# Attention scores in 64x64 TensorE tiles instead of 32x128 ones, and some key products of 480 columns for two of 240

## The chip, the cores and the metric

The kernel runs on one core of a Trainium2 chip. The metric is the device time of one execution in microseconds. Everything is float32, and every matrix product of the program appears in the profile as two TensorE records (two MATMUL and two LDWEIGHTS), so that counts in the profile are twice those in the code. The profile calls the matrix product PE, the loading of its stationary operand ("weights") PEld, VectorE DVE, ScalarE ACT, GpSimd POOL and SyncE SP.

## The reference

There are 16 batches of 100 queries with 640 features, and 8 heads of 80 channels. Each batch attends to 718 keys of 384 features (the first 718 of 722 context rows); the last four rows are extra tokens that get an attention of their own. Cut to what matters here:

```python
query = hidden_states @ Wq                # 16 x 100 x 640
keyt  = enc @ Wk                          # 16 x 718 x 640
valt  = enc @ Wv
scores = einsum('bhqd,bhkd->bhqk', qh, kh) * 80 ** -0.5   # 8 heads of 80 channels
hs = softmax(scores) @ vh
# a second, small attention over the 4 tokens gives ca_hs2
out = (hs + ca_hs2) @ Wout + b_out + hidden_states
```

## The kernel before

**Setup.** `load_heads` (L301) and the DMA behind it (L308, chunk 4) bring the transposed key weights into the room of `kT`, the heads in 32-row pieces, on the DMA queues of ACT and SP. `turn_back` transposes five chunks of 128 channels on TensorE, and `first_keys` makes the keys of batch 0: for each chunk and each 128 features of the context it multiplies three thirds of the keys, 240 columns each (L620). ACT rearranges the query weights from `wq_in` into `wq_sb` with three copies for each of five row chunks (L1279, L1287).

**Channels.** Of each head's 80 channels the first 64 lie in chunks 0 to 3 of `kT` and of the queries `qp`, and the other 16 in chunk 4 (`qz` on the side of the queries). In the kernel before the 64 channels are cut into two pieces of 32 rows: head h has rows 32(h//2) onward of chunks 2(h%2) and 2(h%2)+1. In chunk 4 each head has 16 rows; `qz` holds each query twice with one or the other 16 rows of a 32-row block zeroed, so that one product with 200 columns serves two heads.

**Scores.** For each batch the function `scores` runs three times (groups g = 0, 1, 2), each for two tiles of 120 keys. Inside it, for each key tile and each of the five chunks, four products follow each other, one for each 32-row block r, and each goes to a PSUM bank of its own (L660): stationary are 32 rows x 120 keys of `kT`, moving are 32 rows x 100 queries (chunks 0 to 3) or x 200 columns of `qz` (chunk 4). The four use four separate row tiles of the array (32 rows x 128 columns), and the text below calls four such records with different tiles a quad. Groups 0 and 2 write to two double banks (pool `ps2`), which ACT copies to the tile `st` with one instruction each (L688); group 1 writes to four single banks, copied with four (L682). VectorE takes the running maximum over `st` (`most`: L1416, then `larger`, L1407).

**The rest of a batch.** The order on each engine is the order of the code (the schedule is manual). Behind the scores PE does the small second attention (`z_ps`, `y_ps`), then the values of this batch and the keys of the next in turns (L439, L470: block products that need fewer multiplications, with sums that POOL, DVE and ACT make), while DVE and ACT compute the softmax (`Maximum`, `subtract` L1395, `exponential` L1403). `last_keys` (through `chunk_keys`, L568) makes chunk 4 of the next batch's keys: three thirds of 240 columns times three times 128 features. Every second batch the queries of two batches follow (L544). Then come the products with the probabilities: `r_ps` (L1546, four column tiles of 32) for the last channels of each head and the sum of the probabilities, and `a_ps` (L1564, two column tiles of 64). Behind `a_ps` the next batch's scores follow at once. In batches 1, 3, 5, 11, 13 and 15 an exponential of the second attention (L854) stands on ACT between the copies of group 0 and those of group 1; in batch 0 it stands behind those of group 1.

The lines that the change touches in the product itself:

```python
for a in range(2):
    for c in range(HC):                      # five chunks
        for r in range(RG):                  # four row blocks of 32
            rows = slice(32 * r, 32 * r + 32)
            if c < HC - 1:
                rhs = qp[rows, c // 2, c % 2, (b % 2) * S : (b % 2 + 1) * S]
                product(a, c, rows, r, c // 2 * S, rhs, False)
            else:
                product(a, c, rows, r, 0, qz[rows, 0, b % 2], True)
```

Of the kernel before, what the change touches and what calls it, by code (L numbers as in the profile page):

```python
# [15 lines left out]
NH, D = 8, 80  # L16
# [131 lines left out]
def kernel(  # L148
# [121 lines left out]

    def a_form(enc, f):
        return enc[0][:, A_AT[f]]
# [26 lines left out]
    def load_heads(u):  # L299
        for h in range(u, NH, 2):  # L300
            (nc.scalar, nc.sync)[h // 2 % 2].dma_start(**packed(wkt_sb, wkt, h))  # L301
# [6 lines left out]
    nc.sync.dma_start(  # L308
        out=wkt_sb[:, 4], in_=wkt.rearrange("(h k) n -> h k n", h=NH)[:, 64:]
    )  # L310
# [252 lines left out]
    def chunk_keys(n, banks, weights, enc):  # L563
        copies = []
        for bank, thirds in zip(banks, ((0, 1), (2,))):
            for i, u in enumerate(thirds):
                for c in range(CC):
                    nc.tensor.matmul(  # L568
                        bank[:, i * KT : (i + 1) * KT],
                        weights[c],  # L570
                        a_raw(enc, u, c),
                        start=(i == 0 and c == 0),
                        stop=(c == CC - 1),
                        skip_group_check=True,
                    )
# [21 lines left out]
    def first_keys(enc):  # L597
# [14 lines left out]
        for c, chunks in ((0, (0, 1)), (0, (2, 3)), (1, range(4)), (2, range(4))):  # L612
            if len(banks) < 4 and 2 in chunks:
                for n in (2, 3, 4):
                    turn_back(n, copies[n % 2])
                begin(2, psum1)
                begin(3, psumk)
            for n in chunks:
                for u in range(3):
                    nc.tensor.matmul(  # L620
                        banks[n][u // 2][:, u % 2 * KT : (u % 2 + 1) * KT],
                        wk_sb[:, 2 * c + n % 2, n // 2],
                        a_raw(enc, u, c),
                        start=(u != 1 and c == 0),
                        stop=(c == CC - 1),
                        skip_group_check=True,
                    )
# [8 lines left out]
    def last_keys(b, enc):  # L636
        banks = pair(f"kT_ps_{b}")
        return chunk_keys(
            HC - 1,
            [banks[:, k] for k in range(2)],  # L640
            [wk4[:, c] for c in range(CC)],
            enc,
        )


    def scores(b, g, tiles):
# [11 lines left out]
        def product(a, c, rows, bank, lo, rhs, last):  # L658
            u, j = KC[2 * g + a]
            nc.tensor.matmul(  # L660
                s_ps[bank][:n, 256 * a + lo : 256 * a + lo + rhs.shape[-1]],
                kT[rows, c, u, j * KN : (j + 1) * KN],
                rhs,
                start=bank not in opened,
                stop=last,
                skip_group_check=True,
            )
            opened.add(bank)
# [608 lines left out]
    for c in range(HC):  # L1277
        for u in range(2):
            nc.scalar.copy(  # L1279
                wq_sb[:, c, 2 * u * P : 2 * (u + 1) * P].rearrange(  # L1280
                    "p (v r k) -> p r v k", v=2, r=RG
                ),
                wq_in[c].rearrange("p (r u k) -> p r u k", r=RG, u=2)[
                    :, :, u, :64
                ].rearrange("p r (v k) -> p r v k", v=2),
            )
        nc.scalar.copy(  # L1287
            wq_sb[:, c, 4 * P :].rearrange("p (h k) -> p h k", h=NH),
            wq_in[c].rearrange("p (h k) -> p h k", h=NH)[:, :, 64:],
        )  # L1290
# [56 lines left out]
    last_keys(0, enc)  # L1347
# [29 lines left out]
    for b in range(B):  # L1377
# [55 lines left out]
        if b + 1 < B:  # L1433
# [62 lines left out]
            last_keys(b + 1, enc)  # L1496
# [45 lines left out]
        for i in order:  # L1542
            for e in range(2):
                for h in range(e, NH, 2):
# [4 lines left out]
                        st[i // 2][: KEYS[i], i % 2, h * S : (h + 1) * S],  # L1549
# [11 lines left out]
        for i in range(len(KC)):  # L1561
            for h in range(NH):
# [4 lines left out]
                    st[i // 2][: KEYS[i], i % 2, h * S : (h + 1) * S],  # L1567
# [66 lines left out]
```

## Time and profile before

| | |
|---|---|
| median of 3 runs | 921.77 us (920.55 to 922.27) |
| the profiled execution | 921.04 us, its span 919.3 us |
| PE busy, PEld busy | 912.0 us (99%), 776.6 us (84%) |
| DVE, ACT, POOL busy | 665.5 us (72%), 376.6 us (41%), 620.6 us (68%) |
| granted clock | 1.00 throughout |
| share of the scores (L660) in the chain that ended last | 12% |

The profile gives one execution. The chain that ended last is followed back from the last instruction; the groups by line give busy time and the mean duration of one record; the timeline merges records of one kind that follow each other and gives the start of the first, the time until the end of the last and their count. A record's duration contains the time in the pipeline, so that rates are read here from the distance of starts and not from durations: the scores of batch 1 start at 95.32 us, and the next stage at 102.60 us.

### The profile page before, as it was taken

How to read it: one execution, taken by the hardware profiler on the slowest of the kernel's cores; microseconds unless marked ns; L12 is line 12 of the kernel's file. 1: busy time of each engine (PE TensorE's matmuls, PEld its weight loads, DVE VectorE, ACT ScalarE, POOL GpSimd, SP SyncE). 2: the span in 40 equal slices, each digit the busy share in tenths (PEclk: the TensorE clock that was granted, in tenths of full speed). 3: DMA queues.
4: the chain of work that ended last, by engine and by line, in shares of the span. 5: the costliest groups of instructions: out<-in, count | busy, mean ns of one | idle time of the engine just before them, and what ended most of it. 6: DMA issues, size and time to landing. Idle time of an engine off the chain costs nothing.

```text
span 919.3 us, 26076 instructions
## 1 busy us (share of the span) xinstructions
PE 912.0 (99%) x11155; PEld 776.6 (84%) x11155; DVE 665.5 (72%) x1121; ACT 376.6 (41%) x654; POOL 620.6 (68%) x653
## 2 busy tenths in 40 slices
PE   8999999999999999999999999999999999999998
PEld 8988889797887979888798788988888888888865
DVE  3898795979639696675957759579782887828773
ACT  2354533544324443433434334344541445425351
POOL 9665786677847788476774756755796566955735
PEclk9999999999999999999999999999999999999999
DMA  9604351141402313140221403205140151401312
GB/s 288 218 11 133 66 123 34 29 120 39 103 12 70 106 25 90 43 132 12 72 72 43 132 12 81 71 6 134 43 110 11 34 140 36 111 11 45 86 53 64
DMA packets 68060, 69.50 MB, mean 76 GB/s; under 512 B 25192, under 2 KB 61352, under 8 KB 67944
## 3 DMA queue, kind: packets, MB, share of 16 engines
q1 hardware_dynamic: 67016, 66.97, 27.2%
q8 instruction: 88, 1.44, 0.7%
q10 hardware_dynamic: 464, 0.52, 0.2%
q0 software_dynamic: 464, 0.34, 0.2%
q14 instruction: 28, 0.23, 0.1%
HBM read 62.14 MB, written 8.94 MB: 77 GB/s over the span
## 4 chain that ended last, share of the span: by engine, by line
PE 97%; DMA 1%; POOL 1%; ACT 0%; DVE 0%; issue 0%; ACTq 0%; SPq 0%; DVEq 0%; POOLq 0%
PE s_ps L660 12%; PE v_psA L439 11%; PE v_psB L439 9%; PE k_psA L470 8%; PE a_ps L1564 7%; PE q_ps L544 7%; PE k_psB L470 7%; PE kT_ps L568 6%; PE r_ps L1546 4%; PE v_psC L439 4%; PE k_psC L470 3%; PE y_ps L799 2%; PE v_psD L439 2%; PE o_psy L1128 2%; PE v_psE L439 2%; PE k_psE L470 1%
## 5 line engine op out<-in xcount | busy, mean ns | idle before, releaser
L834 POOL TENSOR_TENSOR e<-ca,g 100x800 f32<-100x800 f32 x60 | 91.8, 1540 | 101.0 <-DVE most L1407 74.3
L439 PE MATMUL v_psA<-wv_sb,enc 128*120 128x320 f32 x384 | 119.6, 434 | 0.0
L507 POOL TENSOR_TENSOR enc<-enc 128x240 f32<-128x240 f32 x144 | 108.7, 765 | 8.0
L439 PE MATMUL v_psB<-wv_sb,enc 128*120 128x320 f32 x320 | 99.2, 432 | 0.0
L660 PE MATMUL s_ps<-qp,kT 32*120 32x100 f32 x3072 | 97.4, 263 | 0.0
L660 PEld LDWEIGHTS s_ps<-qp,kT 32*120 32x120 f32 x3072 | 94.7, 179 | 1.9
L841 POOL TENSOR_TENSOR e<-e,e 100x800 f32<-100x800 f32 x45 | 92.2, 2048 | 3.5
L439 PEld LDWEIGHTS v_psA<-wv_sb,enc 128*120 128x120 f32 x384 | 69.0, 183 | 24.7 <-DVE vs L410 0.9
L1395 DVE TENSOR_TENSOR st<-st,over 120x1600 f32<-120x1600 f32 x46 | 88.8, 1930 | 0.0
L470 PE MATMUL k_psA<-enc,wk_sb 128*128 128x240 f32 x360 | 87.6, 366 | 0.0
L470 PEld LDWEIGHTS k_psA<-enc,wk_sb 128*128 128x128 f32 x360 | 68.4, 190 | 17.1
L1407 DVE TENSOR_TENSOR most<-most,st 120x800 f32<-120x800 f32 x64 | 63.3, 990 | 21.7 <-ACT st L682 20.4
L439 PEld LDWEIGHTS v_psB<-wv_sb,enc 128*120 128x120 f32 x320 | 58.6, 183 | 23.4
L1403 ACT ACTIVATE st<-st 120x1600 f32<-120x1600 f32 x48 | 73.9, 1540 | 8.2 <-DVE st L1395 5.7
L470 PE MATMUL k_psB<-enc,wk_sb 128*128 128x240 f32 x300 | 73.0, 366 | 0.0
L1416 DVE TENSOR_TENSOR most<-st 120x800 f32<-120x800 f32 x16 | 17.3, 1082 | 76.6 <-ACT st L688 76.6
L1564 PE MATMUL a_ps<-st,vs 120*64 120x100 f32 (+1 forms) x1536 | 69.5, 250 | 0.0
L544 PE MATMUL q_ps<-xT,wq_sb 128*128 128x200 f32 x400 | 69.1, 332 | 0.0
L1564 PEld LDWEIGHTS a_ps<-st,vs 120*64 120x64 f32 (+1 forms) x1536 | 66.4, 137 | 2.7 <-issue 2.7
L544 PEld LDWEIGHTS q_ps<-xT,wq_sb 128*128 128x128 f32 x400 | 68.0, 190 | 0.2
L412 ACT COPY vs<-v_psA 120x640 f32<-120x640 f32 x48 | 33.3, 693 | 83.8 <-PE v_psA L439 83.7
L688 ACT COPY st<-s_ps 120x800 f32<-120x800 f32 x64 | 49.7, 829 | 43.4 <-PE s_ps L660 43.4
(183 smaller groups left out, 1886.2 us busy)
## 6 DMA issues: line engine op xcount, KB each, us to landing
pb<-p_d SPq DMA_DIRECT2D x32, 400.0 KB
enc<-in_enct SPq DMA_DIRECT2D x30, 240.0 KB
enc<-in_enct SPq DMA_DIRECT2D x15, 360.0 KB
xT<-in_xt SPq DMA_DIRECT2D x8, 500.0 KB
rest<-in_enct SPq DMA_DIRECT2D x31, 120.0 KB
xn<-in_x SPq DMA_DIRECT2D x11, 320.0 KB
wide_d<-p_d SPq DMA_DIRECT2D x16, 200.0 KB
pb<-wide_d SPq DMA_DIRECT2D x16, 200.0 KB
```

The costliest lines, as they stand in the source:

```text
L439: nc.tensor.matmul(at[0][j][:KN, : H // 2], a_form(self.enc, f)[:, j * KN : (j + 1) * KN], wv_sb[:, W_AT[f]], start=first, stop=last, skip ...
L470: nc.tensor.matmul(at[:, i * KT : (i + 1) * KT], wk_sb[:, W_AT[f], i], a_form(self.enc, f), start=(first and i == 0), stop=last, skip_grou ...
L507: first = nc.gpsimd.tensor_tensor(out, left, right, op)
L544: nc.tensor.matmul(q_ps[:, : 2 * S].rearrange("p (j s) -> p j s", j=2), wq_sb[:, c, n * P : (n + 1) * P], xT[:, :, c, :], start=(c == 0), ...
L568: nc.tensor.matmul(bank[:, i * KT : (i + 1) * KT], weights[c], a_raw(enc, u, c), start=(i == 0 and c == 0), stop=(c == CC - 1), skip_group ...
L660: nc.tensor.matmul(s_ps[bank][:n, 256 * a + lo : 256 * a + lo + rhs.shape[-1]], kT[rows, c, u, j * KN : (j + 1) * KN], rhs, start=bank not ...
L834: first = engine.tensor_tensor(to, self.ca[:, t, :].unsqueeze(1).to_broadcast([S, NH, S]), g[:, :, t].unsqueeze(2).to_broadcast([S, NH, S] ...
L841: engine.tensor_tensor(e, e, to, ALU.add)
L1395: return engine.tensor_tensor(st[i], st[i], top.over[:KN].unsqueeze(1).to_broadcast([KN, 2, ROWS]), ALU.subtract,)
L1403: nc.scalar.activation(st[i], st[i], AF.Exp, scale=SCALE)
L1407: most_now = nc.vector.tensor_tensor(most[:KN], most[:KN], st[i][:, u], ALU.max)
L1564: nc.tensor.matmul(wides[64 * e : 64 * e + 64, h // 2], slot(i, h, FIRST[e], 64), st[i // 2][: KEYS[i], i % 2, h * S : (h + 1) * S], start ...
```

## The change

The first 64 channels of a head now lie together: chunk c holds head 2c in rows 0 to 63 and head 2c+1 in rows 64 to 127. The heads stand in `st` in another order (`PLACE`: first the even heads, then the odd), and the readers of `st` follow it. In `scores` each product with 32 rows x 120 keys becomes one with 64 rows and half of the keys: the stationary operand is 64 rows x 64 keys, or x 56 for the second half, and the four products of a quad use the four 64x64 tiles of the array (two row halves times two column halves). Their number stays: 32 products of 100 columns in a group. The products of chunk 4 keep their form (32 rows x 120 keys, 200 columns, eight in a group), but they no longer stand between those of the key tiles: all products of the heads are together (`heads`), and all of chunk 4 are together (`others`). Groups 0 and 2 do the heads first, group 1 does chunk 4 first, so that the order in a batch is heads, chunk 4 (of groups 0 and 1), heads (of groups 1 and 2), chunk 4.

In `first_keys`, in `last_keys(0)` and in the loop's `last_keys` of batches 6 and 7, the products of the first two thirds of the keys are joined to one with 480 moving columns for the second and third 128 features; the first 128 features stay apart, since one third lies in another tile there. That makes 14 products of 480 columns out of 28 of 240. In the calls of `last_keys` that join, the loop over the features is now the outer one.

In the setup the loads of the key weights go in pieces of 64 rows, the four heads of chunks 0 and 1 first; that of chunk 4 becomes two DMAs on SP's queue instead of one. The query weights take two copies on ACT for each row chunk instead of three.

```diff
+PLACE = [4 * (h % 2) + h // 2 for h in range(NH)]
 def packed(to, w, h):
     rows = w.rearrange("(h k) n -> h k n", h=NH)
-    at, c = 32 * (h // 2), 2 * (h % 2)
-    return {
-        "out": to[at : at + 32, c : c + 2],
-        "in_": rows[h, :64].rearrange("(v k) n -> k v n", v=2),
-    }
+    return {"out": to[64 * (h % 2) : 64 * (h % 2) + 64, h // 2], "in_": rows[h, :64]}
...
     def load_heads(u):
-        for h in range(u, NH, 2):
-            (nc.scalar, nc.sync)[h // 2 % 2].dma_start(**packed(wkt_sb, wkt, h))
+        for h in range(4 * u, 4 * u + 4):
+            (nc.scalar, nc.sync)[h % 2].dma_start(**packed(wkt_sb, wkt, h))
...
-    nc.sync.dma_start(
-        out=wkt_sb[:, 4], in_=wkt.rearrange("(h k) n -> h k n", h=NH)[:, 64:]
-    )
+    for e in range(2):
+        nc.sync.dma_start(
+            out=wkt_sb[64 * e : 64 * e + 64, 4],
+            in_=wkt.rearrange("(c e k) n -> e c k n", e=2, k=D)[e, :, 64:],
+        )
...
+    def a_two(enc, c):
+        at = A_RAW[0, c]
+        return enc[0][:, at : A_RAW[1, c] + 1 : A_RAW[1, c] - at]
...
+    def raw_keys(banks, c, weights, enc, joined=True):
...
+        if joined and (1, c) not in A_REST:
+            product(banks[0], 0, a_two(enc, c), False)
+        else:
+            for u in range(2):
+                product(banks[0], u * KT, a_raw(enc, u, c), u == 0 and c == 0)
+        product(banks[1], 0, a_raw(enc, 2, c), c == 0)
...
-        for a in range(2):
-            for c in range(HC):
+        def heads(last):
+            for a in range(2):
+                for c in range(HC - 1):
+                    for e in range(2):
+                        at = 4 * e + c
+                        rows = slice(64 * e, 64 * e + 64)
+                        rhs = qp[rows, c // 2, c % 2, (b % 2) * S : (b % 2 + 1) * S]
+                        for keys in (slice(0, 64), slice(64, n)):
+                            product(a, c, rows, keys, at // 2, at % 2 * S, rhs, last)
+
+        def others(last):
+            for a in range(2):
                 for r in range(RG):
                     rows = slice(32 * r, 32 * r + 32)
-                    if c < HC - 1:
-                        rhs = qp[rows, c // 2, c % 2, (b % 2) * S : (b % 2 + 1) * S]
-                        product(a, c, rows, r, c // 2 * S, rhs, False)
-                    else:
-                        product(a, c, rows, r, 0, qz[rows, 0, b % 2], True)
+                    product(a, HC - 1, rows, slice(0, n), r, 0, qz[rows, 0, b % 2], last)
+
+        for k, part in enumerate((others, heads) if g == 1 else (heads, others)):
+            part(k == 1)
...
     for c in range(HC):
-        for u in range(2):
-            nc.scalar.copy(
-                wq_sb[:, c, 2 * u * P : 2 * (u + 1) * P].rearrange(
...
+        nc.scalar.copy(
+            wq_sb[:, c, : 4 * P].rearrange("p (h k) -> p h k", h=NH),
+            wq_in[c].rearrange("p (h k) -> p h k", h=NH)[:, :, :64],
+        )
...
-    last_keys(0, enc)
+    last_keys(0, enc, True)
...
-            last_keys(b + 1, enc)
+            last_keys(b + 1, enc, b in (6, 7))
...
-                        st[i // 2][: KEYS[i], i % 2, h * S : (h + 1) * S],
+                        st[i // 2][: KEYS[i], i % 2, PLACE[h] * S : (PLACE[h] + 1) * S],
```

More of the change, by code (lines that the diff above doesn't have):

```diff
@@ L560, in queries, with product, chunk_keys @@
                 )
-    def chunk_keys(n, banks, weights, enc):
-        copies = []
[L565 to L575, printed above, removed]
+    def raw_keys(banks, c, weights, enc, joined=True):
+        def product(bank, lo, rhs, first):
+            cols = rhs.shape[-1] * (rhs.shape[1] if len(rhs.shape) > 2 else 1)
+            to = bank[:, lo : lo + cols]
+            if len(rhs.shape) > 2:
+                to = to.rearrange("p (u k) -> p u k", k=KT)
+            nc.tensor.matmul(
+                to,
+                weights,
+                rhs,
+                start=first,
+                stop=(c == CC - 1),
+                skip_group_check=True,
+            )
[5 more added lines that the diff above has]
+        product(banks[1], 0, a_raw(enc, 2, c), c == 0)
+    def chunk_keys(n, banks, weights, enc, joined):
+        copies = []
+        if joined:
+            for c in range(CC):
+                raw_keys(banks, c, weights[c], enc)
+        else:
+            for bank, thirds in zip(banks, ((0, 1), (2,))):
+                for i, u in enumerate(thirds):
+                    for c in range(CC):
+                        nc.tensor.matmul(
+                            bank[:, i * KT : (i + 1) * KT],
+                            weights[c],
+                            a_raw(enc, u, c),
+                            start=(i == 0 and c == 0),
+                            stop=(c == CC - 1),
+                            skip_group_check=True,
+                        )
         for bank, thirds in zip(banks, ((0, 1), (2,))):
@@ L618, in first_keys @@
             for n in chunks:
[L619 to L627, printed above, removed]
+                raw_keys(banks[n], c, wk_sb[:, 2 * c + n % 2, n // 2], enc)
         for n in banks:
@@ L634, in first_keys, with last_keys @@
                 )
-    def last_keys(b, enc):
+    def last_keys(b, enc, joined=False):
         banks = pair(f"kT_ps_{b}")
@@ L656, in scores, with product @@
         opened = set()
-        def product(a, c, rows, bank, lo, rhs, last):
+        def product(a, c, rows, keys, bank, lo, rhs, last):
             u, j = KC[2 * g + a]
+            first = [k for k in (0, 64) if keys.start <= k < keys.stop and (bank, k) not in opened]
             nc.tensor.matmul(
-                s_ps[bank][:n, 256 * a + lo : 256 * a + lo + rhs.shape[-1]],
-                kT[rows, c, u, j * KN : (j + 1) * KN],
+                s_ps[bank][keys, 256 * a + lo : 256 * a + lo + rhs.shape[-1]],
+                kT[rows, c, u, j * KN + keys.start : j * KN + keys.stop],
                 rhs,
-                start=bank not in opened,
+                start=bool(first),
                 stop=last,
```

16 lines of the change are left out of this document (6 added, 10 removed).

## The prediction

> **What bounds the kernel now.** I read the page first: busy shares and the chain that ended last.
>
> ```profile
> span 919.3 us, 26076 instructions
> ...
> PE 912.0 (99%) x11155; PEld 776.6 (84%) x11155; DVE 665.5 (72%) x1121; ACT 376.6 (41%) x654; POOL 620.6 (68%) x653
> ...
> PE 97%; DMA 1%; POOL 1%; ACT 0%; DVE 0%; issue 0%; ACTq 0%; SPq 0%; DVEq 0%; POOLq 0%
> ```
>
> The chain is PE for 97% of the span: PE's own stream sets the end, and a stage is worth what its records take from start to start. So next the timeline of PE around the scores of batch 1 (start, time to the end of the last, record, count), and the groups by line for the weight loads.
>
> ```profile
> 88.54 0.37 PE L568 MATMUL kT_ps<-rest,wk 128*128 128x240 f32 x1
> 88.83 2.28 PE L1546 MATMUL r_ps<-st,vs 120*32 120x100 f32 x96
> 91.05 4.35 PE L1564 MATMUL a_ps<-st,vs 120*64 120x100 f32 x96
> 95.32 1.10 PE L660 MATMUL s_ps<-qp,kT 32*120 32x100 f32 x32
> 96.24 0.54 PE L660 MATMUL s_ps<-qz,kT 32*120 32x200 f32 x8
> 96.60 1.00 PE L660 MATMUL s_ps<-qp,kT 32*120 32x100 f32 x32
> 97.42 0.54 PE L660 MATMUL s_ps<-qz,kT 32*120 32x200 f32 x8
> ...
> 102.13 0.54 PE L660 MATMUL s_ps<-qz,kT 32*120 32x200 f32 x8
> 102.60 0.75 PE L861 MATMUL z_ps<-y,e 100*32 100x33 f32 x64
> ```
>
> ```profile
> L660 PEld LDWEIGHTS s_ps<-qp,kT 32*120 32x120 f32 x3072 | 94.7, 179 | 1.9
> ...
> L1564 PEld LDWEIGHTS a_ps<-st,vs 120*64 120x64 f32 x1024 | 45.3, 137 | 2.7 <-issue 2.7
> ...
> L1546 PEld LDWEIGHTS r_ps<-st,vs 120*32 120x32 f32 x1024 | 22.6, 110 | 5.7 <-issue 5.0 <-ACT st L1403 0.8
> ...
> L568 PEld LDWEIGHTS kT_ps<-enc,wk 128*128 128x128 f32 x224 | 42.5, 190 | 2.8
> ```
>
> And from the chain in order of time (start, us, records), rows for full-width products and for the last batch:
>
> ```profile
> 32.41 1.69 PE q_ps L544 x10
> ...
> 38.73 6.77 PE q_ps L544 x40
> ...
> 66.39 1.08 PE v_psE L439 x4
> ...
> 85.26 3.65 PE kT_ps L568 x18
> ...
> 104.48 1.10 PE v_psA L439 x4
> ...
> 132.80 3.65 PE kT_ps L568 x18
> ...
> 890.02 1.74 DVE st L1395
> 891.89 7.15 POOL st L1395 x2
> 899.07 1.55 ACT st L1403
> ```
>
> The scores take 102.60 - 95.32 = 7.28 us a batch. A stretch of 32 qp records (8 quads) takes 97.42 - 96.60 = 0.82, so 0.102 a quad: seven spacings of 0.105 and one of 0.085, the latter right behind chunk 4, whose longer stream gave the loads time. What moves in a quad is only 100 columns, and elsewhere such a quad or pair is faster. r_ps is 24 quads from 88.83 to 91.05, 2.22 us; a_ps is 48 pairs from 91.05 to 95.32, 4.27 us. Less the switches below, that is 0.087 and 0.086. Full-width records give the same pace: 200 columns 6.77 / 40 = 0.169, 240 columns 3.65 / 18 = 0.203, 320 columns 1.08 / 4 = 0.270, that is 0.85 ns a column and nearly no offset, so 100 columns are 0.085. The scores thus wait about 0.02 a quad for something else. The loads say for what: their mean goes 110, 137, 179 ns for 32, 64, 120 stationary columns, 0.8 ns a column, so 120 columns occupy a row tile for about 0.100, longer than the 0.085 that the products need; 64 columns take about 0.053.
>
> **The change part by part.**
>
> *Heads, 64x64.* 48 quads a batch as before (3 groups x 32 products x 2 records / 4), each moving 100 columns, but loading at most 64 columns. No 64x64 tile runs in this trace. The bounds are 0.085 (the moving columns) and 0.105 (as now). I take 0.086, a_ps's value: a_ps loads 64 columns into two column tiles beside each other and isn't held up by it, and s_ps shows that row tiles load beside each other too; the change combines the two. 48 x 0.086 = 4.13. That a load runs beside the product before it in the same rows is what a_ps's 0.086 rests on: each of its records uses all rows and brings a load of its own, 0.053 by the columns. [...]
>
> *Chunk 4.* 12 quads of 200 columns, unchanged in form. Two quads now take 96.60 - 96.24 = 0.36, the first of them 0.19; in a row of four or eight I take q_ps's 0.17: 12 x 0.17 = 2.04. At 0.18 it would be 2.15.
>
> *Switching the tile form.* This is what the change adds: heads, chunk 4, heads, chunk 4 have four changes of form behind them in a batch, where the scores had one. Going out costs 0.09 to 0.11: the last kT record starts at 88.54 and r_ps at 88.83, 0.29 where 0.203 is usual; the last chunk-4 stretch takes 102.60 - 102.13 = 0.47 where 0.36 is usual. Coming in costs the first load, which nothing covers: the first qp stretch takes 96.24 - 95.32 = 0.92 against 0.82, so 0.10 for 120 columns; by the columns, 0.05 for 64. Inside a batch: out 4 x 0.11 = 0.44; in, 2 x 0.05 + 2 x 0.10 = 0.30. The way in from a_ps has its going-out share in a_ps's 4.27 before and after, and isn't counted.
>
> *Sum of the scores.* 4.13 + 2.04 + 0.44 + 0.30 = 6.91 against 7.28: 0.37 us less a batch. The faster quads alone save 48 x (0.102 - 0.086) = 0.79, and the three more changes of form give more than half back.
>
> *What the shorter scores run into.* Groups 0 and 2 share their banks, so group 2 waits for two copies; ACT, and DVE's maximum, follow in order:
>
> ```profile
> 98.04 1.55 ACT L688 COPY st<-s_ps 120x800 f32<-120x800 f32 x2 [2.11 <-PE s_ps L660]
> 99.48 0.88 ACT L854 ACTIVATE e<-e 100x800 f32<-100x800 f32 x1
> 100.38 1.68 ACT L682 COPY st<-s_ps 120x400 f32<-120x400 f32 x4
> 102.76 1.55 ACT L688 COPY st<-s_ps 120x800 f32<-120x800 f32 x2 [0.69 <-PE s_ps L660]
> ```
>
> ```profile
> 102.10 2.02 DVE L1407 TENSOR_TENSOR most<-most,st 120x800 f32<-120x800 f32 x2 [1.24 <-ACT st L682]
> ...
> 104.77 2.01 DVE L1407 TENSOR_TENSOR most<-most,st 120x800 f32<-120x800 f32 x2
> ```
>
> The copies of group 0 end at 99.59, and group 2 starts two groups after the first, at 95.32 + 0.92 + 0.36 + 3 x 1.18 = 100.13: 0.54 spare. After the change group 0 ends 2.32 into the stage (heads 0.05 + 16 x 0.086 + 0.11, chunk 4 0.10 + 4 x 0.17), its copies, as long after it as now, at 4.12; group 2 can start at 4.53 (0.68 more of chunk 4, 0.11 out, 0.05 in, 16 x 0.086): 0.41 spare, no wait. In the six batches with L854 there, ACT is full from 98.04 to 102.06, and its copies of group 1, and DVE's next maximum with them, come earlier only by what group 0 gains, 2.46 - 2.32 = 0.14, while PE comes 0.37 earlier. PE has 28 us of values and keys to do (104.48 to 132.80 in this batch) before r_ps needs this softmax, so that costs nothing unless a block product waits for DVE's sums; if that cover is gone, at most the 0.23 in six batches, 1.4 us. In batch 15 the chain does leave PE, for DVE, POOL and ACT (10.4 us in the rows above), and these start from that maximum: there I count 0.1 instead of 0.37. In batch 0 the exponential that z_ps waits for stands behind group 1's copies, which come about 0.6 earlier: 0.2 more than 0.37.
>
> *480 columns for two of 240.* 28 records less. With 0.85 ns a column and an offset of about 2 ns (0.270 for 320 against 0.203 for 240), they save some 2 ns each: 0.06. The upper bound is their loads, 28 x 0.19 = 5.3, if these lay open, but at 0.203 for 240 columns they don't. A moving operand in two pieces costs nothing at q_ps (two pieces of 100, 0.169). The reordered `last_keys` waits for the same double bank.
>
> *Setup.* PE's list of waits, and rows of the timeline:
>
> ```profile
> PE w_ps L589 <- DMA kT<-in_wkt: 0.8, 2, 0.5
> PE m_ps L1321 <- DVE wq L1308: 0.5, 1, 0.5
> ...
> PE z_ps L861 <- ACT e L854: 0.2, 1, 0.2
> ```
>
> ```profile
> 0.82 0.87 SPq L301 DMA_DIRECT2D kT<-in_wkt  x2
> ...
> 4.97 0.78 SPq L308 DMA_DIRECT2D kT<-in_wkt  x1
> ...
> 10.13 0.52 PE L589 MATMUL w_ps<-e,kT 128*128 128x128 f32 x3 [0.50 <-DMA kT<-in_wkt]
> ```
>
> ```profile
> 29.72 0.29 ACT L1287 COPY wq_sb<-wq 128x128 f32<-128x128 f32 x1
> ```
>
> PE stands twice for the key weights, 0.8 in all. Chunk 4 in two DMAs is 2 x 0.435 = 0.87 of issue instead of 0.78, and the second half starts later; whatever SP issues behind it goes 0.1 later. Chunk 0 on the other hand needs two heads instead of four. I take 0, with -0.3 (the wait for the first chunks gone) to +0.5 (the second half lands one issue later). ACT's copies, five fewer, now end at 30.0 and are needed when q_ps starts, at 32.4: nothing.
>
> *Total.* 14 x 0.37 + (0.37 + 0.2) + 0.1 + 0.06 = 5.9. From the profiled execution, 921.04 (the span 919.3 and 1.7 around it), that is 915.1. This execution lies 0.7 below the median of the runs, inside their range, so I predict 915.4.
>
> **The rivals.**
>
> *Column tiles don't load beside each other under row tiles: slower.* If the two column tiles of a row half take turns, 64 + 56 columns are 120 again, and the quad stays at 0.105: heads 48 x 0.105 = 5.04 and the first load 0.10, so the batch is 5.04 + 2.04 + 0.44 + 0.40 = 7.92, 0.64 more, in 15 batches 9.6: 930.6. Where it turns: 0.37 / 48 more than 0.086, that is 0.094 a quad. For it speaks only that this combination is not in the trace; against it a_ps (128 stationary columns in 0.086) and r_ps (four times 32 in 0.087), where turns would need 0.107. 0.10.
>
> [...]
>
> *The gain is eaten by waits and dearer switches.* If each of the four changes of form costs the full 0.11 and 0.10, they take 0.84 instead of 0.74, and 0.27 a batch remains, 16 x 0.27 = 4.3; the waits of the six batches take 1.4 back: 921.04 - 4.3 + 1.4 = 918.1. For it speaks ACT, full in those batches; against it that PE's list of waits has none for DVE or ACT over 0.5 us. 0.10.
>
> *The switches are cheaper between the row-tiled forms.* If nothing drained between tiles of 64 and of 32 rows, the three changes inside a batch would save 0.33 again: 16 x 0.33 = 5.3, 915.4 - 5.3 = 910.1. Both goings-out quoted show the 0.1, so 0.08.
>
> **How the numbers follow.** The forecast has 0.70, with its own range of 913 to 918 (quads at 0.085 or 0.088, chunk 4 at 0.18, setup -0.3 to +0.5). Runs of this kernel spread by 0.2%, about what a measurement can tell from no change. The range reaches over the eaten gain on one side and toward the cheaper switches on the other: 911.5 to 919.5. Faster by more than 0.2% is below 919.9: 0.70 + 0.08 + most of 0.10, so 0.85; slower 0.12; 0.03 remain.
>
> **What would show it.** In the profile after: the scores of a batch take 6.9 us from the first record to z_ps; 64x64 quads start every 0.086; weight loads of 64 columns have a mean near 137 ns; four changes of form with 0.15 to 0.2 each stand between the stretches; kT_ps of batches 6 and 7 keeps 3.6 us with 14 records; q_ps of batch 0 starts at 32.4 as before. It would be wrong if the quads come at 0.1 or more, if z_ps or v_psA wait for ACT's copies, or if the first transposes start much later.

## The result, and the profile after

The changed kernel takes 915.07 us in the median of 6 runs (914.59 to 916.98), the kernel before 921.2 in 6 runs beside it: 0.9938 of its time, with an interval of 0.9928 to 0.9948. It is faster by 0.6%, as forecast, and 0.3 us below the predicted time. The profiled execution took 914.95, its span 913.2 us.

From the page of the profile after: span, busy time, the shares of the chain that ended last, and the weight loads of the scores.

```profile
span 913.2 us, 26025 instructions
...
PE 905.1 (99%) x11127; PEld 756.6 (83%) x11127; DVE 667.6 (73%) x1121; ACT 375.4 (41%) x649; POOL 619.9 (68%) x653
...
PE 94%; DMA 2%; DVE 1%; POOL 1%; ACT 1%; issue 0%; SPq 0%; POOLq 0%; ACTq 0%; DVEq 0%
...
L687 PEld LDWEIGHTS s_ps<-qp,kT 64*56 64x56 f32 (+1 forms) x3072 | 66.9, 130 | 5.9 <-issue 3.9
```

PE's stream still sets the end. The weight loads of the heads' channels have a mean of 130 ns, where those of 120 columns had 179 (the tiles now have 64 or 56). The timeline of PE around the scores of batch 1, in the changed kernel:

```profile
96.25 1.60 PE L687 MATMUL s_ps<-qp,kT 64*64 64x100 f32 x64
97.78 1.63 PE L687 MATMUL s_ps<-qz,kT 32*120 32x200 f32 x32
99.34 2.97 PE L687 MATMUL s_ps<-qp,kT 64*64 64x100 f32 x128
102.24 0.95 PE L687 MATMUL s_ps<-qz,kT 32*120 32x200 f32 x16
103.12 0.83 PE L897 MATMUL z_ps<-y,e 100*32 100x33 f32 x64
```

The scores take 103.12 - 96.25 = 6.87 us instead of 7.28. The four stretches last 1.53, 1.56, 2.90 and 0.88 us from start to start. PE's list of waits after (us in total, how often, the longest):

```profile
PE w_ps L622 <- DMA kT<-in_wkt: 2.3, 2, 1.8
PE idle_ps L1293 <- DVE vaT L1290: 1.1, 1, 1.1
PE m_ps L1352 <- DVE wq L1339: 0.5, 1, 0.5
PE r_ps L1577 <- ACT st L1434: 0.3, 1, 0.3
PE k_ps L1327 <- ACT kT L656: 0.2, 1, 0.2
```

The list of before ended with one more row than the prediction shows:

```profile
PE z_ps L861 <- issue: 0.2, 1, 0.2
```

That is a stall without a cause that the profile names ("issue"). No wait for DVE or ACT is new, and this stall is gone; but the wait for the key weights has grown from 0.8 to 2.3 us. Its place, in the timelines of SP and of PE:

```profile
0.82 1.47 SPq L305 DMA_DIRECT2D kT<-in_wkt  x2
...
5.67 1.26 SPq L313 DMA_DIRECT2D kT<-in_wkt  x2
```

```profile
8.87 0.82 PE L622 MATMUL w_ps<-e,kT 128*128 128x128 f32 x6
11.45 0.52 PE L622 MATMUL w_ps<-e,kT 128*128 128x128 f32 x3 [1.76 <-DMA kT<-in_wkt]
...
48.76 1.43 PE L687 MATMUL s_ps<-qp,kT 64*64 64x100 f32 x56
```

The transposes of chunk 4 start at 11.45 instead of 10.13, `q_ps` of batch 0 at 33.52 instead of 32.24, and the scores of batch 0 at 48.76 instead of 47.49.

Stage by stage, from start to start in the two profiled executions:

| PE's stage | after less before, us |
|---|---|
| setup, up to the scores of batch 0 | +1.27 |
| scores, 16 batches (batch 0 -0.57, each of the others -0.40) | -6.63 |
| `z_ps`, `y_ps` | -0.60, -0.25 |
| values and keys (+0.25 in batch 0), `kT_ps` in the loop | +0.25, -0.02 |
| `r_ps`, `a_ps`, what follows PE's last product | -0.18, +0.13, -0.07 |
| sum | -6.1 |

The scores account for the gain and half a microsecond more. Against them stands the loss in the setup, of which `z_ps` and `y_ps`, two stages that no part of the change touches, give back 0.85.

### The profile page after: what moved, and what is told of

Read it like the earlier page. It is cut to its first block, busy times and chain, and to the rows that moved or that the text cites. A ratio compares the mean times of both kernels' runs of the same rounds, so it can differ in the third digit from the quotient of the medians.

```text
span 913.2 us, 26025 instructions
## 1 busy us (share of the span) xinstructions
PE 905.1 (99%) x11127; PEld 756.6 (83%) x11127; DVE 667.6 (73%) x1121; ACT 375.4 (41%) x649; POOL 619.9 (68%) x653
## 4 chain that ended last, share of the span: by engine, by line
PE 94%; DMA 2%; DVE 1%; POOL 1%; ACT 1%; issue 0%; SPq 0%; POOLq 0%; ACTq 0%; DVEq 0%
PE s_ps L687 12%; PE v_psA L445 11%; PE v_psB L445 9%; PE k_psA L476 8%; PE q_ps L550 7%; PE a_ps L1595 7%; PE k_psB L476 7%; PE kT_ps L601 5%; PE r_ps L1577 4%; PE v_psC L445 4%; PE k_psC L476 3%; PE kT_ps L576 2%; PE y_ps L835 2%; PE v_psE L445 2%; PE v_psD L445 2%; PE o_psy L1164 2%
## 5 line engine op out<-in xcount | busy, mean ns | idle before, releaser
L687 PE MATMUL s_ps<-qp,kT 64*64 64x100 f32 (+1 forms) x3072 | 73.1, 248 | 0.0
L687 PEld LDWEIGHTS s_ps<-qp,kT 64*56 64x56 f32 (+1 forms) x3072 | 66.9, 130 | 5.9 <-issue 3.9
```

What stands on the lines that cost most here:

```text
L687: nc.tensor.matmul(s_ps[bank][keys, 256 * a + lo : 256 * a + lo + rhs.shape[-1]], kT[rows, c, u, j * KN + keys.start : j * KN + keys.stop] ...
```

## The experiments

The theory was that of the prediction: the heads are faster because a 64x64 tile loads 64 columns instead of 120, and the changes of tile form give half of that back. Then two questions came up: what the setup lost, and where the stalls of `z_ps` and `y_ps` come from. All runs were compared with the kernel before on the same chip (medians 920.73 to 921.38).

### Grouping alone: e1

The kernel before with the order of the changed one (heads together, chunk 4 together), in 32x128 tiles.

```diff
-            for c in range(HC):
-                ...
+        def heads(last):  # chunks 0 to 3, 32 rows x 120 keys
+        def others(last):  # chunk 4
+        for k, part in enumerate((others, heads) if g == 1 else (heads, others)):
+            part(k == 1)
```

> The kernel before with one edit: in each group of scores the products of chunk 4 stand together (heads first in groups 0 and 2, chunk 4 first in group 1), as in the change, but all tiles stay 32 rows x 128 columns. Theory (the gain comes from the shorter loads of the 64x64 tiles): the quads of 100 columns stay at 0.105 us, nothing changes form, the scores of a batch stay at 7.2 to 7.3 us and the time within 0.1% of before. Rival (the gain comes from chunk 4 standing together, fewer alternations between 100 and 200 columns): scores near 6.9 us, time near that of the change, 915 us.

921.31 us (920.46 to 922.54), ratio 0.9997 (0.9987 to 1.0006). The timeline of PE in e1, batch 1:

```profile
95.04 1.94 PE L660 MATMUL s_ps<-qp,kT 32*120 32x100 f32 x64
96.80 1.55 PE L660 MATMUL s_ps<-qz,kT 32*120 32x200 f32 x32
98.17 3.52 PE L660 MATMUL s_ps<-qp,kT 32*120 32x100 f32 x128
101.52 0.88 PE L660 MATMUL s_ps<-qz,kT 32*120 32x200 f32 x16
102.32 0.75 PE L868 MATMUL z_ps<-y,e 100*32 100x33 f32 x64
```

102.32 - 95.04 = 7.28, as before. The order is worth nothing; the gain is the tile form's.

### Shorter loads in the old form: e2

The kernel before with chunk 4 first and only 72 of 120 keys in the products of chunks 0 to 3.

```diff
-                kT[rows, c, u, j * KN : (j + 1) * KN],
+                kT[rows, c, u, j * KN : j * KN + n],
...
-            for c in range(HC):
+            for c in (HC - 1, *range(HC - 1)):
...
-                        product(a, c, rows, r, c // 2 * S, rhs, False)
+                        product(a, c, rows, r, c // 2 * S, rhs, c == HC - 2, 72)
```

> The kernel before with 72 instead of 120 stationary keys in the products of chunks 0 to 3 (the scores of the other 48 keys of each tile lack these channels, work left out), still in 32-row x 128-column tiles; chunk 4 is done first in each key tile so that it opens the bank. Theory (the load of 120 columns holds a quad at 0.105): 72 columns load in about 0.06, so quads come every 0.085 to 0.086, scores 7.28 - 0.8 = 6.5 us a batch, time about 921 - 12.8 = 908 us. Rival (the 0.105 belongs to four row tiles or to the issue of eight instructions a quad): quads stay at 0.105, time 921.

913.42 us (912.37 to 914.65), ratio 0.9909 (0.9894 to 0.9924): 5 us more than expected. The undisturbed batches took 6.45 us, 0.82 less than before, and eight quads 0.69, that is 0.086 a quad: with 72 columns the load no longer limits, in the old form either. The 5 us are elsewhere: `z_ps` and `y_ps` took 4.1 us more than in the kernel before, and the scores of five batches 1.6 more than the undisturbed ones. From e2's list of waits, and its timeline of PE at the end of `z_ps` in one batch:

```profile
PE z_ps L861 <- issue: 3.3, 3, 1.5
...
PE y_ps L799 <- issue: 0.8, 2, 0.5
```

```profile
644.42 0.75 PE L861 MATMUL z_ps<-y,e 100*32 100x33 f32 x63
646.69 0.19 PE L861 MATMUL z_ps<-y,e 100*4 100x33 f32 x1 [1.52 <-issue]
```

PE stands for 1.5 us in the middle of a stage, one record before its end, and waits for nothing that the profile names. This is the same kind of stall as the 0.2 of `z_ps` in before's list, and the section on e10 and e12 takes it up.

### Three times the changes of form: e3

The changed kernel with chunk 4 behind the heads of each key tile: twelve changes of form in a batch instead of four.

```diff
-        for k, part in enumerate((others, heads) if g == 1 else (heads, others)):
-            part(k == 1)
+        for a in range(2):
+            heads(a, False)
+            others(a, True)
```

> The changed kernel with chunk 4 behind the heads of each key tile instead of together: twelve changes of tile form a batch instead of four, nothing else. Theory (each change costs a drain of about 0.09 and the first load of 0.05 to 0.10): eight more changes of 0.17 to 0.19 are 1.4 to 1.5 us a batch, scores 8.3 us, time about 915 + 23 = 938 us. Rival (only the drain or only the load is lost): 0.6 to 0.8 us a batch, 925 to 928 us.

937.01 us (936.97 to 937.56), ratio 1.0166 (1.0149 to 1.0183). E3's timeline of PE, batch 1:

```profile
97.09 0.91 PE L687 MATMUL s_ps<-qp,kT 64*64 64x100 f32 x32
97.94 0.61 PE L687 MATMUL s_ps<-qz,kT 32*120 32x200 f32 x8
98.48 0.91 PE L687 MATMUL s_ps<-qp,kT 64*64 64x100 f32 x32
...
105.41 0.75 PE L896 MATMUL z_ps<-y,e 100*32 100x33 f32 x64
```

8.32 us a batch, 1.44 more than in the changed kernel for eight more changes: 0.18 each. So the price of a change of form is real, and the faster tiles in the old order would have been slower than the kernel before.

### What the setup lost: e4, e6, e9, e11

The first guess was that SP issues chunk 4 too late. E4 puts its two DMAs on ACT's queue.

```diff
     for e in range(2):
-        nc.sync.dma_start(
+        nc.scalar.dma_start(
             out=wkt_sb[64 * e : 64 * e + 64, 4],
```

> The changed kernel with the two DMAs of chunk 4's key weights issued from ACT's queue instead of SP's. Theory (the second wait of PE for the key weights in the setup, 1.8 us instead of 0.5, comes from the longer issue on SP): the wait goes to under 0.5, kT_ps of chunk 0 to 3 restarts before 10.5 us, the time falls by 1.2 to 1.8 us against the change, to about 913.5. Rival (the loads are limited by the transfers themselves or another wait follows): time as the change, 915.

916.75 us (915.7 to 919.65), ratio 0.995 (0.9933 to 0.9967): no gain. From e4's timelines of ACT and of PE:

```profile
5.17 1.71 ACTq L313 DMA_DIRECT2D kT<-in_wkt  x2
```

```profile
11.75 0.52 PE L622 MATMUL w_ps<-e,kT 128*128 128x128 f32 x3 [1.43 <-DMA kT<-in_wkt]
```

ACT began to issue at 5.17 instead of 5.67, but took 1.71 us over it where SP took 1.26, so that the issue ended at 6.88 instead of 6.93, and the weights are there no earlier. So e4 did not test what it was made for. What the traces show is that the transposes follow the end of the issue: in the nine traces in which PE waits for chunk 4 they start 4.2 to 4.9 us behind it, in the kernel before at 10.13 behind 5.75 and in the changed one at 11.45 behind 6.93. How much of that distance is transfer, no run here separates.

E6 leaves the DMAs and moves what waits for them: the transposes of chunk 4 behind the first keys of the other chunks.

```diff
-                for n in (2, 3, 4):
+                for n in (2, 3):
...
     first_keys(enc)
+    turn_back(HC - 1, nc.vector.tensor_copy)
```

> The changed kernel, but with the transposes of chunk 4 of the key weights moved behind the first keys of chunks 2 and 3 (PE has 2.6 us more of other work ahead of them). Theory: the 1.27 us that the setup lost is PE's wait for chunk 4 and nothing else; here the wait at 11.45 us goes, the scores of batch 0 start at about 47.3 us instead of 48.76, and the time is 1.3 to 1.8 us below the changed kernel: 913.3 to 913.8. Rival: the setup is bound by what lands later (the context's or the query weights' transfers) or by VectorE's copies behind the transposes, and the wait shows up again under another name: then the scores of batch 0 stay at 48.7 and the time at 915.1.

921.95 us (921.57 to 923.73), ratio 1.0011 (1.0003 to 1.002): 6.2 us above e5, the changed kernel on the same chip, instead of 1.5 below. PE's wait went, but DVE's copy behind the transposes stood in DVE's queue ahead of its sums of the weights. From e6's list of waits of PE, timeline of DVE, and a table of two stretches (the length, PE, PEld, DVE, ACT and POOL busy, then the granted clock, where 1.00 is full speed, the DMA share and GB/s):

```profile
PE m_ps L1353 <- DVE wq L1340: 6.6, 1, 6.6
```

```profile
22.25 0.56 DVE L625 COPY wk<-w_ps 128x384 f32<-128x384 f32 x1 [12.39 <-PE w_ps L622]
```

```profile
28.00:32.00 4.00, 1.31 (x5) 1.32 (x6) 4.00 (x9) 2.13 (x6) 3.77 (x6) 0.57 0.83 256
32.00:36.00 4.00, 4.00 (x20) 4.00 (x19) 2.41 (x5) 0.00 (x0) 3.12 (x5) 0.58 0.18 68
```

DVE waited 12.4 us and PE then 6.6 us for DVE, until 30.7 us. The clock fell to 0.50 inside that wait, at 28.6, and stayed there until 35.4. E9 gives that copy to ScalarE.

```diff
-    turn_back(HC - 1, nc.vector.tensor_copy)
+    turn_back(HC - 1, nc.scalar.copy)
```

> The changed kernel with the transposes of chunk 4 of the key weights behind all first keys, as in e6, but with the copy behind them on ScalarE instead of VectorE, whose queue in e6 stood behind that copy from 9.9 to 22.3 us (its sums of the weights then came late and PE waited 6.6 us for them). Theory: with VectorE's queue free, PE's wait for chunk 4 (1.76 us at 11.45) goes and nothing takes its place; the scores of batch 0 start at 46.8 to 47.4 us instead of 48.76; 913.3 to 914.2 us. Rival: VectorE's sums or the context are late anyway, PE waits for them before m_ps (over 1 us there), and the time stays at 915.

916.78 us (916.12 to 918.5), ratio 0.9957 (0.9945 to 0.9969): still no gain. Neither theory nor rival named the queue that stood now. E9's list of waits of PE, and its timeline of POOL:

```profile
PE y_ps L835 <- POOL m L807: 1.0, 1, 1.0
```

```profile
13.01 0.76 POOL L1300 MEMSET most<- 32x800 f32 x1
22.68 0.76 POOL L1301 MEMSET e<- 32x800 f32 x1 [8.91 <-PE w_ps L622]
```

POOL fills rows of the tile `e` that the transposes read, so it stood until the last transpose, and its sums of the context and the blocks of `m` came late. In the profiled execution (918.5, the longest of the five) the clock fell to 0.50 from 36.9 to 40.3 us behind that wait; the other four, 916.1 to 916.9, have a mean granted clock of 1.00, and they too are no faster than the changed kernel. E11 also moves the fill behind POOL's sums.

```diff
-    nc.gpsimd.memset(e1[96:, :], LOW)
...
     enc_sums(enc)
+    nc.gpsimd.memset(e1[96:, :], LOW)
```

> As e9 (transposes of chunk 4 of the key weights behind the first keys, copy on ScalarE), but GpSimd fills the lower rows of e behind its sums of the context instead of ahead of them. In e9 that fill waited for the transposes (they read the tile), GpSimd stood from 13.8 to 22.7 us, its sums and the block of m behind them came late and PE waited 1.0 us and more for m at y_ps of batch 0, where the clock then fell to 0.50 for 3.4 us. Theory: the wait for chunk 4 is what the setup lost; here it is gone and nothing else waits: y_ps of batch 0 starts at 33.4 us (35.21 in the changed kernel), the scores of batch 0 at 47.0 (48.76), the clock stays at 1.00, and the time is 1.8 us below the changed kernel's 915.1 to 915.8: 913.3 to 914.0, give or take 0.5 for stalls of the instruction fetch. Rival: the setup is bound by transfers (queries' weights, x) that land as late as before: PE waits at q_ps or y_ps again and the time stays at 915.

914.07 us (913.39 to 916.36), ratio 0.9931 (0.9917 to 0.9944). E11's timeline of PE:

```profile
33.52 1.12 PE L835 MATMUL y_ps<-m,xT 128*100 128x96 f32 x10
...
47.07 1.60 PE L687 MATMUL s_ps<-qp,kT 64*64 64x100 f32 x64
```

`y_ps` starts 1.69 us earlier than in the changed kernel (35.21 there), and so do the scores of batch 0: the wait for chunk 4 was all that the setup had lost, and with three queues in order it is got back, with 0.4 more, for the kernel before waited 0.50 there itself. The time is 1.0 us below the changed kernel's first median and 1.7 below that of e5. The intervals of the ratios overlap, so it is the trace that shows this gain and not the time alone (its span is only 1.2 us shorter than the changed kernel's, since `z_ps` has a stall of 0.3 in it). E11 has the lowest median of the kernels here that do all the work.

### The joined products: e5, e7, e8

E5 is the changed kernel again, beside e6 to e8. E7 joins nothing, e8 joins in every batch.

```diff
-    def raw_keys(banks, c, weights, enc, joined=True):
+    def raw_keys(banks, c, weights, enc, joined=False):
...
-    last_keys(0, enc, True)
+    last_keys(0, enc)
...
-            last_keys(b + 1, enc, b in (6, 7))
+            last_keys(b + 1, enc)
```

That is e7; e8 has one line:

```diff
-            last_keys(b + 1, enc, b in (6, 7))
+            last_keys(b + 1, enc, True)
```

> The changed kernel once more, beside the next three on the same chip. Both theories expect its time again, 915.1 us within 1 us, scores of 6.87 us a batch and a wait of about 1.8 us for chunk 4 of the key weights at 11.45 us. The theory that PE's stalls marked "issue" come from the fetching of its instructions in blocks of 256 expects them, if any, at record counts that are 193 or 194 over a multiple of 256; if there are some in this execution, its time is longer by them and not by other rows.

> The changed kernel without any product of 480 columns (all of 240, as in the kernel before), so 56 records more in the setup and batches 6 and 7. Theory: the joins are worth 0.06 us by themselves; the time is that of the changed kernel plus 0.1, 915.2, give or take the 1 us by which the stalls at block bounds can come or go when 56 records shift them. Rival: the loads of the 28 products lie open and the joins hid them, 28 x 0.19 = 5.3 us: 920.4.

> The changed kernel with the joined products in the loop's last_keys of all batches, not of 6 and 7 alone (26 records less). Theory: each joined product saves some 2 ns: 0.05 us in all, 915.0, give or take 1 us for stalls at block bounds. Rival: joining pays (0.19 us of load for each product that falls away, 26 x 0.19 = 4.9 us: 910.2). Second rival: with the loop over the features outside, PE waits for a bank or for a piece of the context in those batches, and the time rises by the sum of the waits before kT_ps, over 1 us.

E5 took 915.79 us (915.07 to 916.17), ratio 0.994 (0.9928 to 0.9952). E7 took 917.14 (916.82 to 919.63), ratio 0.9961 (0.9947 to 0.9974), and e8 919.19 (917.48 to 921.7), ratio 0.9978 (0.9966 to 0.9989). Both are slower than e5 by more than the theory allowed. But not in `kT_ps`: from start to start that stage takes 3.645 us without joins and 3.635 with them in the same batches, so the two joined products of a batch save 0.010. Nor does the other loop order make it wait. The difference stands in the lists of waits, first e7's, then e8's:

```profile
PE z_ps L897 <- issue: 1.1, 2, 0.7
...
PE y_ps L835 <- issue: 0.4, 1, 0.4
```

```profile
PE z_ps L897 <- issue: 1.9, 3, 0.9
...
PE o_ps L1255 <- DVE spare L1128: 0.5, 1, 0.5
...
PE y_ps L835 <- issue: 0.4, 1, 0.4
```

Against the changed kernel's profile, `z_ps`, `y_ps` and the scores take 2.7 us more in e7 and 2.9 in e8, in a few batches; e8 loses 0.8 more in its last stage, where the wait for DVE's `spare` stands, and why it came was not followed up. Edits worth less than 0.1 us by themselves moved the median by 1.4 and 3.4, and the profiled execution by 1.3 and 2.6, with most of the loss where PE waits for nothing that the profile names. Part of e8's median is something else: its four executions of 920.2 and more have a mean granted clock of 0.998, where the others, 917.5 to 919.4, have 0.999 or 1.000. No trace shows where the clock fell in them.

### Instructions in blocks of 256: e10, e12

Packets of 16,384 bytes arrive on a queue that the profile calls "instruction" (87 in the changed kernel, one for about 256 of PE's records, called a block below). Counting PE's records in a trace from the first one, the records before which PE stalls in `s_ps`, `z_ps` or `y_ps` and no semaphore ends the wait have numbers 193 or 194 over a multiple of 256: 46 stalls of 0.18 to 1.7 us from record to record (changes of form, and two records right behind a stall, apart) in fourteen traces (4 in the kernel before, none in the changed kernel's first one and in e3's, 7 in e2's), and no exception. The longer ones (40 of at least 0.3 us from record to record) end 1.2 to 1.6 us after a packet has landed and 3.2 to 4.0 us after PE crossed into the block before. The author's reading of these times, which no run shows by itself, is that a block is fetched while the one before it runs, and that one which runs in less than that ends in a stall. The scores used 256 records in 3.9 us before and use them in 3.7 now; `z_ps` uses its 128 in 0.68. By that reading a block that holds `z_ps` and part of the scores is the shortest, and the stall comes at its end, in `z_ps` or in the `y_ps` behind it (which itself is slow, 20 records in 1.04 us), and which blocks are too short depends on where the bounds fall. How long the stall is differs from one execution to the next: e5 is the changed kernel again and has two stalls where its first trace has none, and e4, with the same instructions on PE, has four. E10 moves the bounds, with products that fill PE's wait at the start.

```diff
         nc.tensor.matmul(idle_ps[:, :P], idle, idle, start=True, stop=True)
+    for _ in range(22):
+        nc.tensor.matmul(
+            idle_ps[:32, :8], idle[:, :32], idle[:, :8], start=True, stop=True
+        )
```

> The changed kernel with 22 more products of 8 columns right behind the seven idle products at its start, where PE waits for the first DMA until 4.28 us. They cost nothing there, but move every later instruction of PE by 88 places against the blocks of 256. Theory of the fetch (a block of 256 takes 2.9 to 3.8 us from the crossing into the one before until PE can use it; a block that PE consumes faster ends in a stall): from the starts of the records in the changed kernel's trace, blocks that are consumed in less than 3.2 us (3.5 us) would wait 0.9 us (3.7) as they lie now and 3.1 us (7.0) moved by 88. So 2.2 to 3.3 us longer: 917.3 to 918.4, the stalls all marked "issue", in s_ps, z_ps and y_ps, at counts of 193 or 194 over a multiple of 256 (counted with the added ones), and all other stages as before. Rival: the place in the stream is chance and the stalls come from other traffic: the time stays at 915.1 within 1 us.

921.35 us (918.77 to 923.18), ratio 1.0005 (0.9995 to 1.0014): the whole gain of the change is gone, more than was expected. E10's list of waits and its timeline of PE, where a bound falls inside `y_ps`:

```profile
PE y_ps L835 <- issue: 1.5, 2, 0.8
PE z_ps L897 <- issue: 1.2, 3, 0.5
```

```profile
272.36 0.75 PE L897 MATMUL z_ps<-y,e 100*32 100x33 f32 x64
273.03 0.42 PE L835 MATMUL y_ps<-m,xT 128*100 128x96 f32 x2
274.23 1.03 PE L835 MATMUL y_ps<-m,xT 128*100 128x128 f32 x8 [0.79 <-issue]
```

In the profiled execution (919.73) the setup is 0.22 longer than in the changed kernel, and `z_ps`, `y_ps` and the scores 1.92, 1.96 and 0.68: 4.6 of the 4.8 us, and 4.4 of them at the same numbers as above. The added products were not free: the first transposes start 1.9 us later, but most of that vanishes in the waits for the key weights. Sign and place are the theory's; the price is not, for the stalled blocks here took 3.2 to 3.9 us and the sum was made with 3.2 to 3.5. The profiled execution is 1.6 us below e10's median, so the trace accounts for 4.8 of the median's 6.3 us over the changed kernel.

E12 does the same to the kernel before, with 14 such products.

> The kernel before with 14 more products of 8 columns behind the seven idle ones at its start: every later instruction of PE lies 56 places further against the blocks of 256. Theory of the fetch, by the starts of the records in the trace of before: blocks consumed in less than 3.2 us (3.5; 3.8) wait 0.3 us (1.4; 4.1) as they lie and 1.5 us (3.6; 7.0) moved by 56, so 1.2 to 2.9 us longer: 922.5 to 924.2, stalls in z_ps and y_ps marked "issue" at counts of 193 or 194 over a multiple of 256, all other stages as in before. Rival: what e10 showed is of the changed kernel alone (its faster scores) or of the added products: then this one stays at 921.3 within 0.5, or its first transposes start later by over 1 us and the loss lies there.

924.07 us (922.89 to 924.98), ratio 1.0035 (1.0021 to 1.0048), at the upper end of what was expected, but only partly for that reason. The stalls moved to new batches, at 193 and 194 again; in sum `z_ps` and `y_ps` took only 0.8 us more, for the stalls of the kernel before went at the same time. E12's timeline of PE:

```profile
7.57 1.17 PE L620 MATMUL kT_ps<-enc,wk_sb 128*128 128x240 f32 x2
```

Here the products at the start were not free, as the rival's last clause had it: the first transposes began 1.2 us later, and the first keys took 1.5 us longer (the two records of this row take 0.67 in before); with that the setup is 2.3 us longer, of 3.5 in the whole span. In e10 the waits for the key weights cover such a delay (1.9 us at the first transposes, 0.22 in the setup). Why that pace was low is not shown; the granted clock in those rows is 1.00. So e12 confirms the places and not the price.

## Why the prediction was right

*The pace of a quad.* Confirmed. Heads were put at 0.086 a quad; the quads in a stretch start every 0.0857. The four stretches of a batch come by the prediction's terms to 1.54, 1.57, 2.91 and 0.89 us; they measure 1.53, 1.56, 2.90 and 0.88. Their sum was put at 6.91 and is 6.87. That shorter loads are the cause is shown by e2, where 72 columns in the old tiles bring 0.086 too, and by e1, where the order alone brings nothing. The rival of column tiles that take turns falls: it would have given 0.105. (Chunk 4 at 0.18 a quad would be 2.16 and not 2.15; nothing hangs on it.) That a load runs beside the product before it in the same rows, which the prediction read from `a_ps`, holds for these tiles too: the two stretches of heads take 1.53 + 2.90 = 4.43 us a batch, their changes of form included, of which 48 quads of 0.0857 are 4.11; loads of 0.053 (the prediction's estimate from its means) that waited for the products would add 48 x 0.053 = 2.5. Of the 0.12 that the prediction gives to slower, 0.10 is that of column tiles in turns; for the other 0.02 no run shows a ground, and the 4.43 us speak against any that lies in the loads.

*The changes of form.* Confirmed by e3: 0.18 each, where the terms (0.11 out, 0.05 to 0.10 in) gave 0.16 to 0.21. The rival of cheaper changes falls with it, and so does the one of dearer changes, which put each at 0.21.

*What the shorter scores run into.* Confirmed in the main: no new wait for ACT or DVE in the list. Batch 0's extra 0.2 measures 0.17, but its values and keys took 0.25 longer, in pauses too short for the list, which the prediction did not count. Batch 15 was put at 0.1; its scores gave 0.40 and `a_ps` took 0.15 back in this execution (in e4, e7 and e10 nothing), so the term was at least 0.15 too small.

*The joined products.* Confirmed: 0.06 was predicted, and 0.010 for two products measured makes 0.07 for fourteen.

*The setup.* Wrong. The term was 0, with +0.5 as its upper bound, and it measured +1.27. The step that failed is the pricing of the DMAs by SP's rows of before (2 x 0.435 = 0.87 of issue for chunk 4, "the second half lands one issue later"): pieces of 64 rows took 1.26 for chunk 4 and 1.47 instead of 0.87 for the first two heads. By the prediction the issue of chunk 4 would have ended 0.1 later; it ended 1.2 later (6.93 instead of 5.75), and the transposes behind it started 1.3 later. Bounds from rows of another shape did not bound it. E11 shows that the wait was the whole loss; why these issues take longer is not shown, and e4 does not tell issue from transfer.

*What the prediction did not have.* Of the stalls of `z_ps` and `y_ps` before's list had one row with 0.2 us, and the prediction passed over it. Start to start, the two stages ran 1.1 us over their shortest in the kernel before and 0.3 in the changed one, whose instructions lie otherwise against the blocks. In e5, the same kernel again, they ran 0.8 over it, so much of this difference belongs to the execution. In the two profiled executions it covered two thirds of what the setup lost. The rest was covered by the scores, which gave 6.63 where their terms made 5.85 (0.40 instead of 0.37 in each batch, and batch 15). That the total came out 0.3 us from the forecast, with one term off by 1.3 and two by 0.8, is luck; that the scores are faster, by about this much and for this reason, is not. E10 shows that the same change with unlucky bounds is worth nothing, and none of the rivals had that cause.

## What to carry to other kernels

Where PE waits for its weight loads, compare the loads per row tile (0.8 ns a column here) with the moving columns (0.85 ns) and choose a tile form that makes the load the shorter one (64 columns instead of 120 took a quad from 0.105 to 0.086 us here), then keep products of one form together, for each change of form cost 0.18 us in e3. When work is moved behind a late transfer, follow every queue that has an instruction tied to it (here DVE's copy, for which PE waited 6.6 us in e6, then POOL's fill of a tile that the transposes read, which stood 8.9 us in e9) before pricing the gain. And in a PE-bound kernel of many short instructions, a difference of a few microseconds between two versions may be where its stalls fall and nothing else (e10's shift by 88 records cost 4.4 us at such places); look for stalls marked "issue" at equal distances, here multiples of 256 records, before explaining it.

## What the runs showed of the hardware

*The stalls at the bounds.* The 46 stalls of `s_ps`, `z_ps` and `y_ps` that no semaphore ends lie at one place, 193 or 194 records over a multiple of 256. In the 40 longer ones PE went on 3.2 to 4.0 us after the crossing into the block before; a packet of 16,384 bytes started on the queue "instruction" 0.5 to 1.7 us after that crossing, took 0.9 to 1.5, and PE went on 1.2 to 1.6 after it had landed. A stall cost up to 1.7 us, and in e10 the stalls at these places cost 4.4 us in all. One block of lead is the author's reading of these times; no run shows more of the fetch than them.

*The clock after a wait.* In e6 the granted clock fell to 0.50 from 28.6 to 35.4 us, beginning 4.4 us into a wait of 6.6. In e9 it fell from 36.9 to 40.3, behind a wait of 1.0 and four shorter ones for the same producer. Behind the 1.76 us for chunk 4 in the changed kernel it did not fall. What makes the difference between the last two is not shown.
